# Cross-attention in fp32 on one core: the first batch loads half of x1 ahead of x2, projects queries ahead of keys, gives every strip of its first scores its own banks, and takes block 11 out of PSUM ahead of T4 and the reciprocal

## The chip, the cores and the metric

The kernel runs on one core of one Trainium2 chip. A core has five engines that run side by side and wait for one another by semaphores: TensorE (PE in the profile; its weight loads are PEld), VectorE (DVE), ScalarE (ACT), GpSimd (POOL) and SyncE (SP), which here only issues DMAs. The metric is the device time of one execution in microseconds (us). The kernel before takes 721.2 us, the median of three runs (721.2 to 721.28).

## What is computed

For each of 8 batches there are two inputs of 512 channels by 1024 positions, `x1` and `x2`. All numbers are fp32.

```python
q = einsum('bcn,dc->bnd', x1, Wq) + bq          # 64 features a position
k = einsum('bcn,dc->bdn', x2, Wk) + bk[:, None]
v = einsum('bcn,dc->bdn', x2, Wv) + bv[:, None]  # 512 channels
attn = softmax(einsum('bnd,bdm->bnm', q, k), axis=2)
return einsum('bcm,bnm->bcn', v, attn) + x1
```

## The kernel before

**The order of the sums.** Since each row of `attn` sums to one, the kernel multiplies `x2` by the unnormalised exponentials first (stage y), divides by the row sums, then multiplies by `Wv` (stage o), and adds `bv` and `x1` on the way out. Both products are cut into 2 by 2 blocks and made with seven block products in place of eight. That costs sums of blocks on DVE: `S1` to `S4` of the left factor (`left_sums`, L100) and `T1` to `T4` of the right factor (`right_sums`, L236). A product accumulates in two pairs of PSUM banks, `a0, a1` and `c0, c1` (table `MULT`, L259). Products 1, 6 and 5 leave their running sum in SBUF as well (tiles `u`, L289). A result block is taken out of PSUM by `evict_y` (L294): for block 11 DVE adds bank pair `c` and `u1` (L303), then multiplies by the reciprocal of the row sums (L306).

**PSUM.** There are eight banks of 128 partitions by 512 numbers: the two pairs `a` and `c`, and two tiles of two banks each in the pool `ps_s`, which serve the scores and the projections in turn.

**The scores.** For each half `h` of the 512-position halves of the queries, `scores` (L164) makes four strips `i` of keys; a strip is two matmuls into a `ps_s` tile or into a named pair of banks. ACT copies each strip to SBUF tile `e` (L187 for a named pair, two copies of 512; L189 for a `ps_s` tile, one copy of 1024). DVE folds the four strips into a running maximum (`fold`, L201), folds the two key halves (L205), and POOL reduces over the partitions (`highest`, L210). DVE then subtracts and ACT takes exponentials. The sums of the exponentials go the same way: folds on DVE, `total` on POOL (L215), the reciprocal on DVE (`shares`, L219).

**The first batch.** `head` (L345) does alone what later periods do for the next batch beside the products. It starts ten warming matmuls on zeros, then loads `wqk`, the four channel chunks of `x2` (L371), and `x1` in four pieces (`load_x1`, L357: two chunks of one position half each). Next come `keys` (bank `c0`), `head_queries` for half 0 (bank `c1`), the loads of `wvT` from ACT's queue (`load_values`, L89), the scores of half 0, the block sums S1 and S2, the queries and scores of half 1, and the exponentials of half 0. Strips 0, 1 and 3 of half 0 use `ps_s`, strip 2 uses pair `a`; DVE folds strips 1 and 3 straight from PSUM.

**The period of batch 0.** `period` (L428) runs product 1 (`first(1)`), finishes the scores of half 1, and then follows a written order: T1, T2, the row sums of half 0, T4, product 2, the reciprocal of half 0, the keys of batch 1, block 11 out of PSUM, and so on. Later, `scores_and(n, 0, "c", ...)` puts strip 2 of the next batch's scores into pair `c`, which block 11 must have left.

**What sets the order.** The kernel is under a manual schedule: each engine runs its instructions in the order in which the code writes them, and waits only for what an instruction reads or overwrites. SP and ACT each have a DMA queue of their own. A DMA also waits on its issuing engine where the semaphore it is given still serves an earlier transfer.

Of the kernel before, what the change touches and what calls it, by code (L numbers as in the profile page):

```python
# [15 lines left out]
def kernel(  # L16
# [69 lines left out]
    def load_values():  # L86
        for r in range(2):
            for k in range(2):
                nc.scalar.dma_start(w[f"{r + 1}{k + 1}"], wvT[r, k])  # L89

    def left_sums(a, *ks):

# [24 lines left out]
    def load_a(s, *ks):  # L117
        for k in ks:
            s.a[k] = sb.tile(
                [P, MH, C // 2], F32, tag=f"a{k}", name=f"a{k}_{s.b}", bufs=1 + (k[0] == "2")  # L120
            )
            nc.sync.dma_start(s.a[k], x2T[s.b, int(k[0]) - 1, int(k[1]) - 1])
# [35 lines left out]
    def keys(s, bank=None):  # L158

        ps = project(s, "k", wk_sb, bank)  # L160
        s.k = sb.tile([P, H], F32, tag="k", name=f"k_{s.b}", bufs=2)
        nc.scalar.activation(s.k, ps, AF.Identity, bias=bk_sb)
# [31 lines left out]
    def fold(s, h, i, kind, op, ps=None):  # L194

        e = s.e[h]
        if i == 1:
            s.mx[h] = sb.tile([P, 2, H], F32, tag="fold", name=f"{kind}_{s.b}_{h}", bufs=2)
        f = s.mx[h]
        new = e[:, :, i, :] if ps is None else ps  # L200
        nc.vector.tensor_tensor(f, e[:, :, 0, :] if i == 1 else f, new, op)  # L201
# [5 lines left out]
    def highest(s, h):  # L207
        fold_halves(s, h, ALU.max)
        s.top[h] = sb.tile([P, H], F32, tag="top", name=f"top_{s.b}_{h}", bufs=2)
        nc.gpsimd.partition_all_reduce(s.top[h], s.mx[h][:, 0, :], P, ReduceOp.max)  # L210
# [6 lines left out]
    def shares(s, h):  # L217
        s.rden[h] = s.den[h]
        nc.vector.reciprocal(s.rden[h], s.den[h])  # L219
# [25 lines left out]
    def sum_e(s, *ks):  # L245
        for i in (0, 2):
            part = {n: v[:, i : i + 2, :] for n, v in s.t.items()}
            for k in ks:
                right_sums(part, k)
# [41 lines left out]

    RESULT = {"11": ("c", 1), "22": ("c", 5), "12": ("a", None), "21": ("c", 6)}

    def evict_y(s, k):  # L294
        bank, add = RESULT[k]
        rden = s.rden[int(k[1]) - 1]
        y = s.y[k] = sb.tile([P, 2, H], F32, tag=f"y{k}", name=f"y{k}_{s.b}")
        for j in range(2):
            ps = s.bank[bank, j]
            if add is None:  # L300
                nc.vector.tensor_tensor(y[:, j, :], ps, rden, ALU.mult)
            else:
                nc.vector.tensor_tensor(y[:, j, :], ps, s.tmp[add, j], ALU.add)  # L303
        if add is not None:
            for j in range(2):
                nc.vector.tensor_tensor(y[:, j, :], y[:, j, :], rden, ALU.mult)  # L306

    def fetch_o(s, k):

# [25 lines left out]
    def head_queries(s, x_sb, h, bank):  # L335

        ps = ps_a.tile([P, H], F32, tag=bank, name=f"ps_q_{s.b}_{h}")
        for c in range(CT):
            for r in (lo, hi):
                nc.tensor.matmul(  # L340
                    ps[r, :], wq_sb[:, c, :], x_sb[:, c, ts(h, H)], start=(c == 0), stop=(c == CT - 1)
                )
        nc.scalar.activation(s.q[:, ts(h, H)], ps, AF.Identity, bias=bq_sb)  # L343

    def head(s):  # L345

        s.q = sb.tile([P, N], F32, tag="q", name=f"q_{s.b}", bufs=2)
        x1_sb = sb.tile([P, CT, N], F32, tag="x", name="x1_head")
        x2_sb = sb.tile([P, 2, MH, H], F32, tag="e1", name="x2_head")
        s.x = x2_sb.rearrange("p a (b t) n -> p (a b) (t n)", t=2)

        def load_x1(queue, c, h):
            queue.dma_start(  # L357
                x1_sb[:, c : c + 2, ts(h, H)],
                x1[s.b, c * P : (c + 2) * P, ts(h, H)].rearrange("(t p) n -> p t n", p=P),
            )  # L360

        nc.gpsimd.dma_start(bqk_sb, bqk)
        nc.gpsimd.dma_start(bv_sb, bv)
        nc.scalar.dma_start(wqk_sb, wqk)
        warm = const.tile([P, P], F32, name="warm")
        nc.vector.memset(warm, 0.0)
        ps = ps_a.tile([P, H], F32, tag="a0", name="ps_warm")
        for _ in range(WARM):
            nc.tensor.matmul(ps[:, 0:P], warm, warm, start=True, stop=True)
        for c, queue in ((0, nc.sync), (1, nc.sync), (2, nc.scalar), (3, nc.sync)):  # L370
            queue.dma_start(s.x[:, c, :], x2[s.b, ts(c, P), :])  # L371
        load_x1(nc.scalar, 0, 0)
        load_x1(nc.sync, 2, 0)
        nc.scalar.activation(warm[:, 0:1], warm[:, 0:1], AF.Exp)
        load_a(s, "11")
        load_x1(nc.sync, 0, 1)
        load_x1(nc.sync, 2, 1)
        load_a(s, "21", "22", "12")
        keys(s, "c0")
        head_queries(s, x1_sb, 0, "c1")  # L380
        load_values()
        copies = [scores(s, 0, i, "a" if i == 2 else None) for i in range(MH - 1)]
        for copy in copies:
            copy()
        fold(s, 0, 1, "max", ALU.max, copies[1].ps)
        copy = scores(s, 0, 3)
        fold(s, 0, 3, "max", ALU.max, copy.ps)
        copy()
        fold(s, 0, 2, "max", ALU.max)
        highest(s, 0)  # L390
        sum_a(s, "S1", "S2")
        head_queries(s, x1_sb, 1, "c0")
        load_x(states[1], x1)
        copies = [scores(s, 1, 0), scores(s, 1, 1), scores(s, 1, 2, "c")]
        for g in range(2):
            for i in range(MH):
                first_exponentials(s, g, i)
        for copy in copies:
            copy()
        fold(s, 0, 1, "sum", ALU.add)  # L400
        fold(s, 0, 2, "sum", ALU.add)
        fold(s, 1, 1, "max", ALU.max)
        fold(s, 0, 3, "sum", ALU.add)
# [24 lines left out]
    def period(s, n, nn, nnn):  # L428

        def first(i):
            multiply(s, "y", i, s.a, s.t, MH)

        def second(i):
            multiply(s, "o", i, w, s.y, 2)

        open_t(s)
        first(1)
        if s.b == 0:  # L440
            head_second(s, n)
        sum_e(s, "T1", "T2")
        if s.b == 0:
            total(s, 0)
        sum_e(s, "T4")
        if n:
            load_a(n, "11")
        first(2)
        shares(s, 0)
        if s.b == 0:  # L450
            keys(n)
            load_x(nn, x1)
        evict_y(s, "11")
        sums(s, 1)
        sum_e(s, "T3")
        shares(s, 1)
        if n:
            load_a(n, "12", "21", "22")
        first(6)

        def next_queries():
            queries(nn)
            load_x(nn, x2)

        def next_keys():
            keys(nn)
            if nnn:
                load_x(nnn, x1)

        if n:  # L470
            scores_and(n, 0, "c", next_queries if nn else nothing)
            for i in range(1, MH):
                fold(n, 0, i, "max", ALU.max)
            highest(n, 0)
            if s.b == 0:
                left_sums(w, "S1", "S2", "S3", "S4")
        first(5)
        fetch_o(s, "11")
        fetch_o(s, "22")
        if n:  # L480
            for i in range(MH):
                exponentials(n, 0, i)
            if s.b:
                sum_a(n, "S1", "S2", "S3")
        first(7)
        evict_y(s, "22")
        first(3)
        evict_y(s, "12")
        if n:
            scores_and(n, 1, "a", next_keys if nn else nothing)  # L490
            sums(n, 0)
        sum_y(s, "T1")
        sum_y(s, "T2")
        if n:
            sum_a(n, *(("S4",) if s.b else ("S1", "S2", "S3", "S4")))
            for i in range(1, MH):
                fold(n, 1, i, "max", ALU.max)
            highest(n, 1)
        first(4)
        evict_y(s, "21")  # L500
        second(1)
        sum_y(s, "T3")
        sum_y(s, "T4")
        second(6)
        fetch_o(s, "12")
        if n:
            exponentials(n, 1, 0)
            exponentials(n, 1, 1)
        second(2)
        evict_o(s, "11")  # L510
        fetch_o(s, "21")
        second(5)
        if n:
            exponentials(n, 1, 2)
            exponentials(n, 1, 3)
        second(7)
        evict_o(s, "22")
        if n:
            second(3)
            evict_o(s, "12")  # L520
            second(4)
            evict_o(s, "21")
        else:
            second(4)
            evict_o(s, "21")
            second(3)
            evict_o(s, "12")
# [37 lines left out]
```

## Time and profile before

| what | us |
|---|---|
| median of three runs | 721.2 |
| the profiled execution, its own time | 720.54 |
| its span, first to last instruction | 718.5 |
| PE busy, of the span | 706.5 |
| DVE busy, of the span | 591.7 |
| POOL busy, of the span | 98.4 |
| TensorE clock granted, mean | 0.999 of full |

The page was taken from one profiled execution. Its time is 2.04 us more than its span; this is what lies before the first and after the last instruction. A busy engine is not the bound by that alone: what counts is which stretch an engine stands idle in, and what ended the wait. In a timeline line, the first number is the start, the second the busy time of the merged instructions, and the bracket holds the idle time of the engine before them with the instruction or transfer that ended it. The DMA engines move 332 GB/s on average in the first 16 us, and the loads of the first batch keep them busy until about 22 us.

### The profile page before, as it was taken

The numbers are of one execution on the slowest core, as the hardware profiler recorded it, in microseconds if no ns is written. First come the engines' busy times: TensorE is split into PE (matmuls) and PEld (weight loads), VectorE is DVE, ScalarE is ACT, GpSimd is POOL, SyncE is SP. The second block draws the span as 40 slices with busy tenths as digits, with TensorE's granted clock in tenths as the row PEclk, the third lists the DMA queues.
The fourth block names the chain that finished last, engine by engine and source line by source line (L and its number), as shares of the span: only waits on it lengthen the run. The fifth ranks groups of instructions, "written<-read, shape, count | busy, mean of one in ns | idle before, by whom it ended". The sixth has DMA issues, their size and how long they took to land.

```text
span 718.5 us, 5410 instructions
## 1 busy us (share of the span) xinstructions
PE 706.5 (98%) x1892; PEld 299.3 (42%) x1892; DVE 591.7 (82%) x569; ACT 201.6 (28%) x270; POOL 98.4 (14%) x38
## 2 busy tenths in 40 slices
PE   7899999999999999999999999999999999999997
PEld 3333444434444444444344443443434444444443
DVE  0999999887969889798887988879887898989444
ACT  2644323033230432115221242312324033230010
POOL 0124120030300302002110202002020020301100
PEclk9999999999999999999999999999999999999999
DMA  9566332243433413435033351332601350042003
GB/s 340 201 194 236 126 146 103 92 149 111 146 118 136 144 56 146 147 117 190 12 136 145 118 191 69 116 136 90 219 0 59 117 176 0 0 157 78 0 1 146
DMA packets 34699, 87.39 MB, mean 122 GB/s; under 512 B 3953, under 2 KB 3953, under 8 KB 34673
## 3 DMA queue, kind: packets, MB, share of 16 engines
q1 hardware_dynamic: 32352, 82.85, 32.8%
q10 hardware_dynamic: 2256, 4.20, 1.7%
q8 instruction: 15, 0.25, 0.1%
q14 instruction: 12, 0.09, 0.1%
q0 software_dynamic: 64, 0.00, 0.0%
HBM read 68.42 MB, written 16.78 MB: 119 GB/s over the span
## 4 chain that ended last, share of the span: by engine, by line
PE 86%; DVE 8%; DMA 3%; issue 1%; ACT 1%; ACTq 0%; DVEq 0%
PE ps_ya L279 27%; PE ps_yc L279 20%; PE ps_oa L279 14%; PE ps_oc L279 12%; PE ps_s L180 5%; PE ps_q L138 3%; PE ps_k L138 2%; DVE max L201 2%; DMA x_head<-in_x_dram 1%; DVE e L230 1%; DVE eT L236 1%; DMA o<-in_x_dram 1%; DVE aS L100 1%; PE ps_sc L180 1%; PE ps_sa L180 1%
## 5 line engine op out<-in xcount | busy, mean ns | idle before, releaser
L215 POOL PARTITION_ALL_REDUCE den<-sum x16 | 66.2, 4136 | 431.7 <-DVE sum L205 431.7
L279 PE MATMUL ps_ya<-eT,aS 128*128 128x512 f32 x256 | 113.1, 595 | 0.0
L279 PE MATMUL ps_yc<-e,a 128*128 128x512 f32 x256 | 112.6, 592 | 0.0
L289 ACT COPY uy<-ps_ya 128x512 f32<-128x512 f32 x48 | 28.1, 588 | 231.2 <-PE ps_ya L279 231.2
L230 DVE TENSOR_TENSOR e<-e,top 128x1024 f32<-128x1024 f32 x60 | 69.9, 1216 | 11.9 <-POOL top L210 11.9
L279 PEld LDWEIGHTS ps_ya<-eT,aS 128*128 128x128 f32 x256 | 48.0, 190 | 63.8 <-issue 62.8
L279 PEld LDWEIGHTS ps_yc<-e,a 128*128 128x128 f32 x256 | 48.6, 190 | 61.6 <-issue 60.1
L320 DVE SCALAR_TENSOR_TENSOR o<-ps_oc,bv_sb,o 128x512 f32<-128x512 f32 x48 | 35.8, 749 | 42.2 <-PE ps_oc L279 42.0
L231 ACT ACTIVATE e<-e 128x1024 f32<-128x1024 f32 x60 | 62.3, 1056 | 25.3 <-DVE e L230 23.5
L189 ACT COPY e<-ps_s 128x1024 f32<-128x1024 f32 x48 | 47.5, 1025 | 63.4 <-PE ps_s L180 61.8
L289 ACT COPY uo<-ps_oa 128x512 f32<-128x512 f32 x48 | 28.1, 585 | 131.0 <-PE ps_oa L279 127.7
L279 PE MATMUL ps_oc<-y,w 128*128 128x512 f32 x128 | 57.6, 593 | 0.3 <-DVE y L306 0.3
L279 PE MATMUL ps_ya<-e,a 128*128 128x512 f32 x128 | 56.3, 593 | 1.3 <-ACT e L225 1.3
L279 PE MATMUL ps_oa<-yT,w_S 128*128 128x512 f32 x128 | 57.5, 592 | 0.0
L279 PE MATMUL ps_yc<-eT,a 128*128 128x512 f32 x128 | 57.0, 598 | 0.0
L279 PE MATMUL ps_ya<-e,aS 128*128 128x512 f32 x128 | 56.2, 592 | 0.0
L219 DVE RECIPROCAL den<-den 128x512 f32<-128x512 f32 x16 | 53.6, 3349 | 0.0
L180 PE MATMUL ps_s<-q,k 64*128 64x512 f32 x192 | 49.5, 607 | 1.6 <-ACT q L343 1.6
L210 POOL PARTITION_ALL_REDUCE top<-max x16 | 30.6, 1914 | 135.5 <-DVE max L205 135.5
L303 DVE TENSOR_TENSOR y<-ps_yc,uy 128x512 f32<-128x512 f32 x48 | 31.1, 674 | 15.9 <-PE ps_yc L279 15.9
L201 DVE TENSOR_TENSOR sum<-sum,e 128x1024 f32<-128x1024 f32 x32 | 39.2, 1225 | 2.1
L201 DVE TENSOR_TENSOR max<-max,e 128x1024 f32<-128x1024 f32 x31 | 38.0, 1225 | 3.1
(66 smaller groups left out, 758.5 us busy)
## 6 DMA issues: line engine op xcount, KB each, us to landing
x_in_x_dram<-in_x_dram SPq DMA_DIRECT2D x56, 512.0 KB, 5.6
a<-in_x2T_dram SPq DMA_DIRECT2D x32, 512.0 KB, 4.3
o<-in_x_dram SPq DMA_DIRECT2D x64, 256.0 KB, 6.5
out_dram<-o SPq DMA_DIRECT2D x64, 256.0 KB, 2.1
x_head<-in_x_dram SPq DMA_DIRECT2D x6, 512.0 KB, 8.8
q<-q ACTq DMA_DIRECT2D x14, 128.0 KB, 7.2
x_head<-in_x_dram ACTq DMA_DIRECT2D x2, 512.0 KB, 8.5
w<-in_wvT_dram ACTq DMA_DIRECT2D x4, 256.0 KB, 5.6
```

What stands on the lines that cost most here:

```text
L138: nc.tensor.matmul(ps[r, :], w_sb[:, c, :], s.x[:, c, ts(h, H)], start=(c == 0), stop=(c == CT - 1),)
L180: nc.tensor.matmul(ps[g], s.k[r, ts(i, P)], s.q[r, ts(h, H)], start=True, stop=True)
L189: nc.scalar.copy(e[:, :, i, :], whole)
L201: nc.vector.tensor_tensor(f, e[:, :, 0, :] if i == 1 else f, new, op)
L215: nc.gpsimd.partition_all_reduce(s.den[h], s.mx[h][:, 0, :], P, ReduceOp.add)
L219: nc.vector.reciprocal(s.rden[h], s.den[h])
L230: nc.vector.tensor_tensor(e, e, top, ALU.subtract)
L231: nc.scalar.activation(e, e, AF.Exp)
L279: nc.tensor.matmul(ps, left[ka][:, k, ts(j, P)], right[kb][:, k, :], start=opens and k == 0, stop=i in (2, 3, 4) and k == n_k - 1, skip_gr ...
L289: nc.scalar.copy(s.tmp[i, j], ps)
L303: nc.vector.tensor_tensor(y[:, j, :], ps, s.tmp[add, j], ALU.add)
L320: nc.vector.scalar_tensor_tensor(o, s.bank[bank, j], bv_sb[:, c : c + 1], o, ALU.add, ALU.add)
```

## The change

Four things are edited, all of them in the first batch.

- `load_values` issues the four `wvT` loads on SP instead of ACT, and is called ahead of the projections.
- `head` loads half 0 of `x1` ahead of `x2`, deals the chunks of `x2` out to SP and ACT in turn, and projects the queries of half 0 ahead of the keys.
- The strips of half 0 go to `ps_s`, `ps_s`, pair `a` and pair `c`. The copy of strip 1 on ACT moves behind those of strips 2 and 3; DVE folds strip 1 from PSUM after the first copy, then strips 2 and 3 from SBUF. The queries of half 1 go to bank `a0` instead of `c0`.
- In the period of batch 0, the keys of batch 1 and the next load of `x1` are written ahead of DVE's work; DVE takes block 11 out of PSUM (the sums with `u1`), then makes T4, then the reciprocal, and then multiplies block 11 by it. `evict_y` gets a list of steps for this. Other batches keep their order.

```diff
@@ load_values
-                nc.scalar.dma_start(w[f"{r + 1}{k + 1}"], wvT[r, k])
+                nc.sync.dma_start(w[f"{r + 1}{k + 1}"], wvT[r, k])
@@ evict_y
-    def evict_y(s, k):
+    def evict_y(s, k, steps=(1, 2)):
+
         bank, add = RESULT[k]
-        rden = s.rden[int(k[1]) - 1]
-        y = s.y[k] = sb.tile([P, 2, H], F32, tag=f"y{k}", name=f"y{k}_{s.b}")
-        for j in range(2):
-            ps = s.bank[bank, j]
-            if add is None:
-                nc.vector.tensor_tensor(y[:, j, :], ps, rden, ALU.mult)
-            else:
-                nc.vector.tensor_tensor(y[:, j, :], ps, s.tmp[add, j], ALU.add)
-        if add is not None:
+        rden = s.rden.get(int(k[1]) - 1)
+        if 1 in steps:
+            s.y[k] = sb.tile([P, 2, H], F32, tag=f"y{k}", name=f"y{k}_{s.b}")
+        y = s.y[k]
+        for step in steps:
             for j in range(2):
-                nc.vector.tensor_tensor(y[:, j, :], y[:, j, :], rden, ALU.mult)
+                ps = s.bank[bank, j]
+                if add is None:
+                    if step == 1:
+                        nc.vector.tensor_tensor(y[:, j, :], ps, rden, ALU.mult)
+                elif step == 1:
+                    nc.vector.tensor_tensor(y[:, j, :], ps, s.tmp[add, j], ALU.add)
+                else:
+                    nc.vector.tensor_tensor(y[:, j, :], y[:, j, :], rden, ALU.mult)
@@ head
-        for c, queue in ((0, nc.sync), (1, nc.sync), (2, nc.scalar), (3, nc.sync)):
-            queue.dma_start(s.x[:, c, :], x2[s.b, ts(c, P), :])
         load_x1(nc.scalar, 0, 0)
         load_x1(nc.sync, 2, 0)
+        for c, queue in ((0, nc.sync), (1, nc.scalar), (2, nc.sync), (3, nc.scalar)):
+            queue.dma_start(s.x[:, c, :], x2[s.b, ts(c, P), :])
...
         load_a(s, "21", "22", "12")
+        load_values()
+        head_queries(s, x1_sb, 0, "c1")
         keys(s, "c0")
-        head_queries(s, x1_sb, 0, "c1")
-        load_values()
-        copies = [scores(s, 0, i, "a" if i == 2 else None) for i in range(MH - 1)]
-        for copy in copies:
-            copy()
+        copies = [scores(s, 0, i, bank) for i, bank in enumerate((None, None, "a", "c"))]
+        copies[0]()
         fold(s, 0, 1, "max", ALU.max, copies[1].ps)
-        copy = scores(s, 0, 3)
-        fold(s, 0, 3, "max", ALU.max, copy.ps)
-        copy()
+        for i in (2, 3, 1):
+            copies[i]()
         fold(s, 0, 2, "max", ALU.max)
+        fold(s, 0, 3, "max", ALU.max)
         highest(s, 0)
         sum_a(s, "S1", "S2")
-        head_queries(s, x1_sb, 1, "c0")
+        head_queries(s, x1_sb, 1, "a0")
@@ period
         if s.b == 0:
             total(s, 0)
-        sum_e(s, "T4")
+        else:
+            sum_e(s, "T4")
         if n:
             load_a(n, "11")
         first(2)
-        shares(s, 0)
         if s.b == 0:
             keys(n)
             load_x(nn, x1)
-        evict_y(s, "11")
+            evict_y(s, "11", (1,))
+            sum_e(s, "T4")
+            shares(s, 0)
+            evict_y(s, "11", (2,))
+        else:
+            shares(s, 0)
+            evict_y(s, "11")
```

## The prediction

> **What bounds the kernel now.** I read the busy time by stages first, because the page's average (PE 98% busy) hides where PE stands idle. The columns are the stage, its length, and the busy time of PE, PEld, DVE, ACT and POOL.
>
> ```profile
> core 0: us, PE busy (x) PEld busy (x) DVE busy (x) ACT busy (x) POOL busy (x), PEclk, DMA share, GB/s
> 0.00:16.00 16.00, 11.79 (x53) 5.78 (x53) 0.17 (x1) 2.86 (x4) 1.60 (x6) 1.00 0.89 332
> 16.00:28.23 12.23, 10.13 (x44) 3.60 (x45) 8.81 (x9) 5.29 (x8) 2.68 (x1) 1.00 0.80 289
> 28.23:52.09 23.86, 23.67 (x71) 8.73 (x72) 23.50 (x24) 15.17 (x21) 2.69 (x1) 1.00 0.49 158
> 52.09:110.43 58.34, 56.97 (x159) 23.18 (x157) 57.40 (x52) 18.88 (x25) 16.16 (x5) 1.00 0.48 167
> 110.43:714.40 603.97, 603.96 (x1568) 258.06 (x1568) 501.07 (x486) 159.44 (x214) 75.28 (x26) 1.00 0.31 107
> 714.40:718.50 4.10, 0.00 (x0) 0.00 (x0) 0.75 (x1) 0.00 (x0) 0.00 (x0) 0.90 0.39 146
> ```
>
> From 110.43 to 714.40 PE has no idle time. All that can be won lies before 110.43: 16.00 − 11.79 = 4.21 us, then 2.10, 0.19 and 1.37. Next I read PE's timeline for what ended those waits.
>
> ```profile
> 1.05 4.04 PE L369 MATMUL ps_warm<-warm 128*128 128x128 f32 x20 [1.05 <-DVE warm L366]
> ...
> 11.56 3.65 PE L340 MATMUL ps_q<-x_head,wqk_sb 128*64 128x512 f32 x16 [0.61 <-DMA x_head<-in_x_dram]
> 16.00 1.99 PE L180 MATMUL ps_s<-q,k 64*128 64x512 f32 x8 [0.79 <-ACT q L343]
> ...
> 28.23 7.13 PE L279 MATMUL ps_ya<-e,a 128*128 128x512 f32 x16 [1.31 <-ACT e L225]
> ...
> 60.99 1.29 PE L180 MATMUL ps_sc<-q,k 64*128 64x512 f32 x3 [0.90 <-DVE y L303]
> ```
>
> Two more waits follow, 0.17 us at 90.03 and 0.31 us at 110.43, both for DVE (L301, L306). The chain of waits says why: from 17 to 110 us it runs mostly over DVE, and DVE is busy 57.40 of 58.34 us in the fourth stage. So **up to 16 us the loads bound the kernel, then DVE's backlog until 110.43, then PE.** A PE wait that goes before 110.43 is a gain only if DVE also gets through earlier; otherwise PE waits at 90.03 or 110.43 instead.
>
> **Part 1: loads and projections.** Before, the keys are done as chunks land, and the queries wait for `x1`: they start at 11.56, ACT starts on them at 15.26 for 0.69, and scores start at 16.00. Afterwards one piece of `x1` is first on SP, the other second on ACT behind `wqk`. By packets, the two queues share evenly: from 3 to 5 us q1 (SP) moved 154 packets and q10 (ACT) 132, but 0.57 MB against 0.24 MB, as SP's were 4 KB and ACT's 2 KB; from 9.5 to 10.5, both at 2 KB, it was 0.20 against 0.20 MB. The Trainium skill (DMA: Bandwidth & Descriptors, Queues, rings and completion order) has the engines alternate between queues by packet, which fits. It also says under "Issuing engines are not separate DMA queues" that issuing from several engines saves only issue time. By that rule dealing `x2` to both queues gains nothing; by the rows it decides who is first, since packet size weighs. I take the rows. Both queues have moved 0.13 and 0.01 MB by 3.0 us. At 0.20 MB/us SP has its 0.524 MB at 4.97. ACT then has 0.40 of the 0.786 MB it needs, and gets a third of 0.40 MB/us against SP's 4 KB packets: 0.386 / 0.133 = 2.9 us, so 7.87. A landing follows the last byte by 0.5 (before, ACT's first 0.786 MB were moved at 7.85 and landed at 8.34): 8.36. The queries start at 8.40, 3.16 us earlier.
>
> But the keys now stand behind them. Sixteen matmuls, from the row's starts (0.48 after the first, then 0.427) and 0.59 for the last, end 7.05 us later, and ACT starts 0.05 after: 15.50. Adding 0.69 and 0.05, **scores start at 16.24, 0.24 later than now.** The last chunk of `x2` comes at about 13.5 by the same shares, and is needed at 14.4, so it hides with 0.9 to spare. The bound of this step: 0.5 either way for the landing (16.24 ± 0.5).
>
> `load_values` takes 1.80 us of ACT's queue away (15.27 to 17.07). Nothing is gained: the first score copy starts at 17.18, when its matmuls end. On SP the four issues go ahead of the next batch's `x1`, which waits for the queries of half 1 (23.33) anyway. SP's issues can wait for semaphores of earlier transfers, but those land by about 20. The `w` tiles are read at 79.10, so the cover is wide; if SP were late, the next `x1` landed at 31.9 and is used at 36.35: 4 us of slack.
>
> **Part 2: the strips.** Let S be the start of the scores. Now ACT copies strips 0 and 1 (17.18, 1.93 us), and DVE's first fold starts at 19.13 = S + 3.13, since it waits for ACT to leave strip 1's banks. Afterwards it follows copy 0 alone: S + 1.18 + 0.97 = S + 2.17. Strip 2's two copies (0.55 each, the first when its matmul ends, S + 2.45) end at S + 3.58. Fold 2 is then at S + 3.60, fold 3 one pace of 1.33 later, the fold of halves another 1.26: S + 6.19, against 23.05 = S + 7.05. **Gain 0.86.** Strip 3's copies (to S + 4.7) and strip 1's (to S + 5.7) hide under the queries of half 1; bank `a0` is free at S + 3.0 and needed at S + 3.6. POOL's reduction, S1, S2 and the exponentials follow in unchanged order, so `first(1)` starts 0.86 − 0.24 = 0.62 earlier. PE is ready then: its scores end at 26.91 + 0.24 = 27.15, and 28.23 − 0.62 = 27.61. DVE's backlog moves by 0.62 with it.
>
> **Part 3: block 11.** No instruction is added or dropped; five groups change places on DVE.
>
> ```profile
> 52.69 4.40 DVE L236 TENSOR_TENSOR eT<-e,eT 128x1024 f32<-128x1024 f32 x2
> 52.86 4.14 POOL L215 PARTITION_ALL_REDUCE den<-sum  x1 [10.36 <-DVE sum L205]
> ...
> 57.03 3.35 DVE L219 RECIPROCAL den<-den 128x512 f32<-128x512 f32 x1
> 60.30 1.22 DVE L303 TENSOR_TENSOR y<-ps_yc,uy 128x512 f32<-128x512 f32 x2
> ```
>
> T4's two instructions take 4.40 us where two such take 2.44 elsewhere: single records show 1.22 and 3.26, so the second loses 2.04 us to POOL. At 108.50 the two additions of a PSUM bank take 1.28 while POOL's reduction (108.75, 1.78) runs, and that reduction is as long as with DVE idle. So the block's additions should pass beside POOL where T4 does not. Where a 1024-wide sum is in flight at POOL's start, POOL takes longer (2.68 against 1.78 for the maximum), as if each held the other out. From that: POOL holds DVE for 2.0 us, starting at 53.0 when nothing is in its way. Additions 52.69 to 53.97; T4's first waits to 55.0 and ends at 56.2, the second at 57.3; reciprocal to 60.6; products to 61.8. Now the next fold starts at 62.65, then at 61.73. **Gain 0.92 on DVE**; bounds 0.0 (additions slowed as T4 is) and 1.2 (T4 not held at all). I take 0.92, as the row at 108.50 is the nearest.
>
> PE no longer waits 0.90 at 60.99, arrives 0.90 earlier at 90.03 and 110.43, and finds DVE 0.92 earlier: the small waits stay as they are. So PE's and DVE's gains are the same time, not two. The keys of batch 1 and `load_x`, written earlier, pass only DVE instructions: PE's, ACT's and SP's own orders do not change (16 matmuls, one activation, four DMAs), and POOL's queue has nothing between.
>
> **The sum:** −0.62 − 0.92 = −1.5 us. Span 718.5 to 717.0, the execution's own 720.54 to 719.0; the median is 0.66 us above the profiled execution, and 721.2 becomes **719.7**.
>
> **A rule against it.** PE now idles from 5.09 to 8.40, 3.3 us, where the longest gap was 1.34. The row: after the last matmul (714.39) the granted clock falls to half at 717.69, 3.3 us later; it rose at 4.30, 3.25 us after the first. The Trainium skill (TensorE: Matmul & The Clock Gate, What's actually happening) has a free-running window of 3.4 us, and an idle one halves the clock. The full-clock stretch, 713.39 us, is 209 such windows, so edges lie at 4.30, 7.71 and 11.13; the window up to 7.71 has 0.79 us of warming in it. By the rule it isn't idle and the sum stands; by the bare 3.3 us of the row the clock falls, the queries run at half speed for one window, and 1.6 us go.
>
> **Rivals.**
> - *Clock down for one window:* −1.5 + 1.6, 721.3. For: the gap is as long as the one at the end. Against: the 0.79 us. 0.15.
> - *Clock down for two windows,* through queries and keys: 3.4 us lost, 723.1. This is the slower side; it decides once PE loses over 3 us before the scores, as would a landing of `x1` at its old 11.51. 0.13.
> - *Block 11 gains nothing,* POOL holding the additions as well: −0.6, 720.6. 0.10.
> - *`x1` lands at 7.5 and T4 is held less:* −2.6, 718.6. 0.12.
> - *As summed,* 719.7 ± 0.6: 0.50.
>
> 0.2% is 1.44 us, about what a measurement can tell: faster means below 719.76. The main case gives 0.27 faster and 0.23 same; with 0.12 from the early case, faster is 0.39. Same: 0.23 + 0.10 + 0.11 of the one-window case = 0.44. Slower: 0.13 + 0.04 = 0.17. The range, 718.9 to 721.6, leaves out the two-window case and the ends.
>
> **What would show it.** Queries at about 8.4 with matmuls 0.43 apart (0.85 if the clock fell) and scores at 16.2; the first fold 2.2 us after them, `first(1)` at 27.6; the additions of block 11 at 0.6 to 0.7 each under POOL's reduction, no PE wait for L303, and the small waits at L301 and L306 still there. A clock below full before 16 us, a late `x2` chunk, or additions of 2 us would prove the sum wrong.

## The result and the profile after

The changed kernel takes 724.14 us, the median of six runs (723.28 to 724.74), against 721.2 before (six runs, 720.78 to 721.59). The ratio is 1.004, with a 95% interval of 1.0027 to 1.0053: 0.4% slower, where 719.7 was forecast. The profiled execution took 724.10 us, its span is 722.1; before it was 720.54 and 718.5. Four of the six executions show a mean granted clock of 0.995 and took 724.1 to 724.7; the other two show 0.999 and took 723.3 and 723.4, still over 2 us more than before. The trace is of one of the four, so where the other two lose is not shown.

The first view is again the busy time by stages. The stages are cut at the same events as before: the start of the scores, of product 1, of DVE's fold of the row sums ahead of T4, and of the product that follows PE's last wait.

```profile
core 0: us, PE busy (x) PEld busy (x) DVE busy (x) ACT busy (x) POOL busy (x), PEclk, DMA share, GB/s
0.00:20.47 20.47, 14.32 (x52) 7.45 (x52) 0.17 (x1) 2.86 (x4) 1.59 (x6) 0.83 0.91 338
20.47:32.22 11.75, 10.13 (x44) 3.60 (x44) 8.82 (x9) 5.35 (x9) 2.68 (x1) 1.00 0.47 157
32.22:56.08 23.86, 23.79 (x71) 8.91 (x72) 23.51 (x23) 15.17 (x21) 2.69 (x1) 1.00 0.50 163
56.08:113.62 57.54, 55.95 (x159) 22.72 (x157) 56.57 (x52) 18.48 (x25) 15.26 (x5) 1.00 0.47 169
113.62:717.60 603.98, 603.95 (x1568) 258.06 (x1568) 501.10 (x486) 159.34 (x214) 75.24 (x26) 1.00 0.31 107
```

By length, the first stage grew from 16.00 to 20.47 us (+4.47), the second shrank from 12.23 to 11.75 (−0.48), the third did not move, and the fourth shrank from 58.34 to 57.54 (−0.80). The fifth is the same to 0.01 us; the tail grew by 0.4. So the two parts on DVE gained, and apart from the tail everything that was lost was lost before the scores. The clock column says where to look: 0.83 in the first stage.

PE's timeline of the changed kernel:

```profile
1.04 4.47 PE L373 MATMUL ps_warm<-warm 128*128 128x128 f32 x20 [1.04 <-DVE warm L370]
9.84 6.42 PE L344 MATMUL ps_q<-x_head,wqk_sb 128*64 128x512 f32 x16 [4.33 <-DMA x_head<-in_x_dram]
16.08 3.62 PE L138 MATMUL ps_k<-x_head,wqk_sb 128*64 128x512 f32 x16
20.47 1.99 PE L180 MATMUL ps_s<-q,k 64*128 64x512 f32 x8 [0.78 <-ACT k L162]
...
93.21 1.29 PE L180 MATMUL ps_sa<-q,k 64*128 64x512 f32 x3 [1.27 <-DVE y L306]
```

Two things are new. PE waits 4.33 us for `x1`, which lands at 9.71. And the same sixteen query records that took 3.65 us before take 6.42. In the keys after them the pace is normal again. The rows below show why. They are cut where the recorded clock changes, at 5.21, 8.62 and 15.45 us. The first two changes are 3.41 us apart and the last two twice that, so the cuts are made every 3.41 us; the stretches between them are called windows here.

```profile
1.79:5.20 3.41, 3.41 (x18) 3.41 (x17) 0.00 (x0) 1.28 (x1) 0.85 (x2) 1.00 0.84 231
5.21:8.61 3.40, 0.30 (x3) 0.11 (x1) 0.00 (x0) 0.20 (x1) 0.00 (x0) 1.00 1.02 393
8.63:12.03 3.40, 2.19 (x6) 0.86 (x8) 0.00 (x0) 0.00 (x0) 0.00 (x0) 0.50 1.03 417
12.04:15.43 3.39, 3.39 (x10) 1.06 (x8) 0.00 (x0) 0.00 (x0) 0.00 (x0) 0.50 1.03 391
15.45:18.86 3.41, 3.41 (x18) 1.25 (x16) 0.00 (x0) 0.69 (x1) 0.00 (x0) 1.00 1.03 408
```

After the length, the first number is PE's busy time, and the third from the end is the granted clock. In the second window PE worked 0.30 of 3.40 us, and the clock is at half for the two windows that follow. It returns after the window in which PE was busy throughout; the one before it, with 2.19 of 3.40 us, did not bring it back. The 1.00 of the first row is no measurement, since the clock has no record before 5.21 us: its 18 warming records are the pace of half speed. The run with 28 warming matmuls, e1_bridge, passes 16 in the window before its first record (1.22 to 4.61) and 32 in the one behind it (4.63 to 8.03). Half speed ahead of the first record is thus not counted in the mean clock. The two executions at 0.999 may be ones in which the clock first rose during the queries; this is not shown.

### The profile page after: what moved, and what is told of

The parts are those of the page before. It is cut to its first block, busy times and chain, and to the rows that moved or that the text cites. A ratio compares the mean times of both kernels' runs of the same rounds, so it can differ in the third digit from the quotient of the medians.

```text
span 722.1 us, 5409 instructions
## 1 busy us (share of the span) xinstructions
PE 708.1 (98%) x1892; PEld 300.7 (42%) x1892; DVE 590.9 (82%) x569; ACT 201.2 (28%) x271; POOL 97.5 (13%) x38
## 4 chain that ended last, share of the span: by engine, by line
PE 86%; DVE 10%; issue 1%; DMA 1%; ACT 1%; ACTq 0%; DVEq 0%
PE ps_ya L279 27%; PE ps_yc L279 20%; PE ps_oa L279 14%; PE ps_oc L279 11%; PE ps_s L180 5%; PE ps_k L138 3%; PE ps_q L138 2%; DVE max L201 2%; DVE e L230 1%; DMA x_head<-in_x_dram 1%; DVE eT L236 1%; DVE aS L100 1%; PE ps_sa L180 1%; DVE den L219 1%; PE ps_q L344 1%
## 5 line engine op out<-in xcount | busy, mean ns | idle before, releaser
L180 PE MATMUL ps_s<-q,k 64*128 64x512 f32 x188 | 47.9, 608 | 1.6 <-ACT q L347 0.8
L308 DVE TENSOR_TENSOR y<-ps_yc,uy 128x512 f32<-128x512 f32 x48 | 31.2, 675 | 15.9 <-PE ps_yc L279 15.9
```

Of the source, the lines that this page charges most:

```text
L180: nc.tensor.matmul(ps[g], s.k[r, ts(i, P)], s.q[r, ts(h, H)], start=True, stop=True)
```

## The experiments

All of them were timed against runs of the kernel before on the same chip, which had medians of 720.8 to 720.9. Differences below are taken to those, unless another kernel is named.

**Each part alone.** Part 3 (block 11) and part 2 (strips), each put into the kernel before, and both together. Their diffs are the parts of the change shown above; nothing else is edited.

> The kernel before with part 3 alone (keys of batch 1 written earlier; block 11 out of PSUM, T4, reciprocal, products). My theory: DVE's next fold 0.8 earlier, the PE wait of 0.90 for L303 gone, 720.4 (0.1% faster). Rival (PE and DVE only swap waits, 1.27 us appears at L306): no gain, 721.2.

> The kernel before with part 2 alone (four pairs of banks for the strips, first fold after the first copy, queries of half 1 in bank a0). My theory: scores at 16.0 as before, fold of halves at 22.6 and first(1) at 27.75, 0.48 earlier, 720.7. Rival (strip copies in two pieces and the queries' new bank cost what the earlier fold gains): first(1) at 28.2, 721.2.

> The kernel before with parts 2 and 3, loads and projections untouched. If the gains add (both move DVE's backlog, which is the bound until 110 us): 0.48 + 0.82 = 1.3, so 719.9 and 0.18% faster. If they are the same time twice: 720.4. If the changed kernel's loss lies in these parts: 722 or more.

| run | us | against before | ratio, 95% interval |
|---|---|---|---|
| block 11 alone | 720.03 | −0.87 | 0.9989 (0.9982 to 0.9995) |
| strips alone | 720.37 | −0.53 | 0.9993 (0.9985 to 1.0001) |
| both | 719.59 | −1.31 | 0.9983 (0.9976 to 0.9989) |

The gains add: 0.87 + 0.53 = 1.40, measured 1.31. (The interval of the strips alone touches 1; that part rests on the sum and on the traces.) So they are not the same time counted twice. What the changed kernel loses, it loses in the rest, part 1 and the `wvT` loads: 724.14 − 721.2 + 1.31 = 4.25 us. This is a subtraction; part 1 was not run alone.

**The clock.** The changed kernel with more warming matmuls, so that PE is busy while it waits for `x1`: 28 in e1_bridge, 18 in e6_warm18, 22 in e10_warm22.

```diff
-    WARM = 10
+    WARM = 28
```

> The changed kernel with 28 warming matmuls in place of 10, so that PE stays busy until x1 lands at about 9.7. Clock theory (the half-speed queries, 9.84 to 16.08 where 3.5 us are enough, cost 2.8 us): clock full from about 5 us on, queries in 3.5 to 3.7 us, scores at about 17.7, time 2.8 below the changed kernel, about 721.3, the same as before within 0.2%. Landing theory (the late x1 and the last chunk of x2 at 14.5 set the end, the clock is hidden): scores stay at 20 or later and the time stays at about 724.

> The changed kernel with 18 warming matmuls: they end at about 7.2, PE then idles 2.5 to 3.3 us. If the clock falls only after a window with next to no PE work, it stays full and the time is that of the bridged kernel, 721.8. If a window that is mostly idle is enough, the queries run at half speed in some executions and the median is 722.5 or more.

> The changed kernel with 22 warming matmuls alone: the partner of the run with one-chunk pieces. Two-chunk pieces on both queues: x1 at 9.7 to 10.6 as in the three profiles so far, queries 0.9 to 1.8 us later than with one-chunk pieces and the time as much longer: 721.0 to 722.0. If the late landing was chance, both runs have the same time.

With 28 the time is 721.79 us (ratio to before 1.001, 1.0002 to 1.0018), with 22 it is 721.39 (1.0009, 1.0001 to 1.0017): 2.4 to 2.8 us below the changed kernel's 724.14, or 2.1 to 2.4 when each is taken against its own runs of the kernel before. In the trace with 28, `x1` came even later:

```profile
1.05 8.21 PE L373 MATMUL ps_warm<-warm 128*128 128x128 f32 x56 [1.05 <-DVE warm L370]
10.69 3.65 PE L344 MATMUL ps_q<-x_head,wqk_sb 128*64 128x512 f32 x16 [1.43 <-DMA x_head<-in_x_dram]
14.14 3.63 PE L138 MATMUL ps_k<-x_head,wqk_sb 128*64 128x512 f32 x16
18.55 1.99 PE L180 MATMUL ps_s<-q,k 64*128 64x512 f32 x8 [0.78 <-ACT k L162]
```

The queries take 3.65 us again and the scores start 1.92 us earlier than in the changed kernel, although the queries began 0.85 later. The profiled execution is 1.91 us shorter too (722.19 against 724.10). So the clock theory holds, though the scores came at 18.55 and not at 17.7, as `x1` landed later still. The landing theory falls as the whole of the cause: PE's time through the queries is not hidden by the last chunk of `x2`.

With 18 matmuls the median is 722.05 us (1.002, 1.0013 to 1.0027), but the 17 executions lie in groups from 721.1 to 723.8. The profiled one, at 723.51, bounds the share of work that keeps the clock:

```profile
6.93:10.33 3.40, 1.19 (x11) 1.00 (x9) 0.00 (x0) 0.20 (x1) 0.00 (x0) 1.00 1.04 414
10.35:13.74 3.39, 3.37 (x8) 1.11 (x10) 0.00 (x0) 0.00 (x0) 0.00 (x0) 0.50 1.02 402
13.76:17.16 3.40, 3.40 (x18) 1.24 (x16) 0.00 (x0) 0.69 (x1) 0.00 (x0) 1.00 1.05 399
```

A window in which PE was busy 1.19 of 3.40 us, 35%, was followed by half speed, though PE's gap inside it was only 2.25 us. In the kernel with both DVE parts (e4_both) a window of 1.71 of 3.40 us, 50%, was followed by full speed:

```profile
4.44:7.84 3.40, 1.71 (x10) 0.71 (x9) 0.00 (x0) 0.20 (x1) 0.00 (x0) 1.00 0.84 292
7.86:11.25 3.39, 2.94 (x12) 0.66 (x12) 0.00 (x0) 0.00 (x0) 0.00 (x0) 1.00 1.03 404
```

**The landing.** With the clock full, the changed kernel is still 1.9 to 2.2 us behind the two DVE parts (0.55 to 0.89 above the kernel before, against 1.31 below it), and its `x1` lands at 9.71, 10.55, 10.24 and 10.06 us in the four traces with 10, 28, 18 and 22 warming matmuls, where 8.36 was forecast. Two theories were tested: the form of the transfer (two chunks in one, on both queues at once) and the length of its rows.

```diff
-        load_x1(nc.scalar, 0, 0)
-        load_x1(nc.sync, 2, 0)
+        for c, queue in ((0, nc.scalar), (2, nc.sync), (1, nc.scalar), (3, nc.sync)):
+            queue.dma_start(x1_sb[:, c, ts(0, H)], x1[s.b, ts(c, P), ts(0, H)])
```

This is e5_pieces, with 28 warming matmuls, and e9_pieces22, with 22.

> The changed kernel with 28 warming matmuls, and half 0 of x1 in four transfers of one chunk (256 KB, still rows of 2 KB) instead of two of two chunks, two on each queue. Form theory (a transfer of two chunks starts slowly): queries start at about 8.4, time 2 us below the bridged kernel, 719.7. Row theory (rows of 2 KB are delivered at a limited number a microsecond at the start, whatever the form): queries start at 9.7 to 10.7, 721.3 to 722.

> The changed kernel with half 0 of x1 in four transfers of one chunk, and 22 warming matmuls, which end before x1 is there (in e5 the 28 ended at 10.4 and held the queries, though x1 had landed at 8.8). Form theory: the last piece lands at 8.8, queries start at about 8.9, scores at 16.7, time 719.9 to 720.3. Row theory: the last piece lands at 9.7 or later again and the time is 721 or more.

In e5_pieces the last piece lands at 8.77, but the time is 721.34 (1.0006, 0.9998 to 1.0014): in the profiled execution the clock rose late, at 7.06, so the warming ran to 10.41 and held the queries. With 22 the last piece lands at 8.76 and the time is 719.67 (0.9985, 0.9978 to 0.9991), 1.72 us below its partner e10_warm22. Here are the two, first with one-chunk pieces, then with two-chunk pieces.

```profile
8.50 3.65 PE L344 MATMUL ps_q<-x_head,wqk_sb 128*64 128x512 f32 x16
11.98 3.60 PE L138 MATMUL ps_k<-x_head,wqk_sb 128*64 128x512 f32 x16
16.38 1.99 PE L180 MATMUL ps_s<-q,k 64*128 64x512 f32 x8 [0.79 <-ACT k L162]
```

```profile
10.20 3.65 PE L344 MATMUL ps_q<-x_head,wqk_sb 128*64 128x512 f32 x16 [1.92 <-DMA x_head<-in_x_dram]
13.65 3.63 PE L138 MATMUL ps_k<-x_head,wqk_sb 128*64 128x512 f32 x16
18.06 1.99 PE L180 MATMUL ps_s<-q,k 64*128 64x512 f32 x8 [0.78 <-ACT k L162]
```

The scores start 1.68 us earlier, which is the 1.72. Of the 1.70 us between the starts of the queries, 1.30 is the later landing (10.06 against 8.76); the rest is that with one-chunk pieces the first queries need not wait for the last piece. Same bytes, same rows, same queues: the form decides between these two. How it does so is not settled. What the traces show is a hole on ACT's queue behind `wqk`. These are the packets of the two queues (q1 is SP's, q10 ACT's; packets, MB, share of the DMA engines) from 4 to 5 us in the changed kernel:

```profile
q1 hardware_dynamic: 100, 0.20, 71.3%
q10 hardware_dynamic: 7, 0.01, 3.2%
```

Both pieces of `x1` had been issued by 1.65 us, yet ACT's queue moved 7 packets where SP's moved 100; the even share that the sum relied on had nothing to share. From 5 us on ACT's piece flowed. The other three traces of two-chunk pieces have the hole from 4.5 to 5.5 us, and the one-chunk traces do not have it. Here is that microsecond, first in e10_warm22 and then in e9_pieces22:

```profile
q1 hardware_dynamic: 141, 0.33, 88.0%
q10 hardware_dynamic: 37, 0.04, 13.2%
```

```profile
q10 hardware_dynamic: 117, 0.23, 58.1%
q1 hardware_dynamic: 89, 0.17, 48.0%
```

A two-chunk piece on ACT does not make the hole by itself. In e8_between, below, the same piece stands behind `wqk` on ACT, but SP's queue begins with whole rows of `x2`: in that microsecond ACT moved 49 packets against SP's 64, and the piece landed at 8.86.

The row theory was tried with whole rows of `x1`, with 28 warming matmuls. Two whole chunks are as many bytes as four half ones, so the queries of half 0 of batch 0 use chunks 0 and 1 twice and leave out chunks 2 and 3. This kernel does not compute the result, and serves for its time alone.

```diff
-                    ps[r, :], wq_sb[:, c, :], x_sb[:, c, ts(h, H)], start=(c == 0), stop=(c == CT - 1)
+                    ps[r, :], wq_sb[:, c, :], x_sb[:, c if h else c % 2, ts(h, H)], start=(c == 0), stop=(c == CT - 1)
...
-        load_x1(nc.scalar, 0, 0)
-        load_x1(nc.sync, 2, 0)
+        nc.scalar.dma_start(x1_sb[:, 0, :], x1[s.b, ts(0, P), :])
+        nc.sync.dma_start(x1_sb[:, 1, :], x1[s.b, ts(1, P), :])
...
-        load_x1(nc.sync, 0, 1)
+        load_x1(nc.sync, 2, 0)
```

> The changed kernel with 28 warming matmuls, and as many bytes of x1 ahead of x2, but as two chunks in whole rows of 4 KB instead of four chunks in half rows of 2 KB; batch 0's queries of half 0 use chunks 0 and 1 twice and leave out chunks 2 and 3. Row theory: x1 is there by 7.5 to 8.5, scores at 16.2 or PE-bound earlier, about 2 us below the bridged kernel. Queue theory (the piece behind wqk on ACT waits for the descriptors of SP's, whatever the rows): queries still start at 9.7 or later.

The time is 721.14 us (1.0005, 0.9997 to 1.0014) and the piece on ACT lands at 9.09, between what the two theories expected. The run is inconclusive on rows. With the same 28 warming matmuls, rows of 2 KB in one-chunk pieces landed earlier (8.77, e5_pieces) than rows of 4 KB, so long rows are not what an early landing needs.

**Another order.** Part 2 and part 3 kept, but `x1` between the chunks of `x2`, so that PE always has something to do. The edit is shown against the kernel before; the `wvT` loads stay on ACT.

```diff
-        for c, queue in ((0, nc.sync), (1, nc.sync), (2, nc.scalar), (3, nc.sync)):
-            queue.dma_start(s.x[:, c, :], x2[s.b, ts(c, P), :])
+        for c in (0, 1):
+            nc.sync.dma_start(s.x[:, c, :], x2[s.b, ts(c, P), :])
         load_x1(nc.scalar, 0, 0)
         load_x1(nc.sync, 2, 0)
+        for c, queue in ((2, nc.scalar), (3, nc.sync)):
+            queue.dma_start(s.x[:, c, :], x2[s.b, ts(c, P), :])
...
-        keys(s, "c0")
+        head_keys(0, 1)
         head_queries(s, x1_sb, 0, "c1")
+        head_keys(2, 3)
```

`head_keys` runs the matmuls of `keys` for the named chunks into bank `c0`; the activation follows the last. The second run has 14 warming matmuls in place of 10.

> Parts 2 and 3 with another order of loads and projections: x2 chunks 0 and 1, then half 0 of x1, then x2 chunks 2 and 3; keys of chunks 0 and 1, queries, keys of chunks 2 and 3. 4 KB rows are first and PE has work while x1 comes. My estimate from the queue shares: x1 at 8.8 and 9.9, queries 8.9 to 12.4, keys done at 14.1, scores at 14.9 to 15.7, so 0.5 to 1.3 us below parts 2 and 3 alone. Rival (ACT's queue again holds its x1 piece to 11 us): scores at 16.3 or later, no gain or a loss.

> The kernel of e8 with 14 warming matmuls in place of 10. In e8 two of eight executions took 719.8 at a mean clock of 0.997, as if the clock had fallen once. If a window less than half busy is the cause, four more warming matmuls (about 0.9 us) fill it: no such executions, median 718.7 to 718.9. If they delay the first keys, up to 0.5 us is lost.

The times are 718.82 us (0.9975, 0.9965 to 0.9985) and 718.28 (0.9967, 0.9954 to 0.9979): faster than both kernels. PE's timeline of the second:

```profile
6.72 1.94 PE L390 MATMUL ps_k_head<-x_head,wqk_sb 128*64 128x512 f32 x8
8.84 3.65 PE L344 MATMUL ps_q<-x_head,wqk_sb 128*64 128x512 f32 x16 [0.19 <-DMA x_head<-in_x_dram]
12.33 1.89 PE L390 MATMUL ps_k_head<-x_head,wqk_sb 128*64 128x512 f32 x8
15.00 1.99 PE L180 MATMUL ps_s<-q,k 64*128 64x512 f32 x8 [0.79 <-ACT k L399]
```

From 6.72 us PE stands idle only 0.19 us until the last key, and the scores start at 15.00, 1.0 us earlier than before and 1.4 earlier than in e4_both (16.36), which is the 1.31 us between them. The two executions of e8 at 719.8 and a clock of 0.997 have no counterpart in the five of e11. With so few executions, that the clock is their cause is not proven.

## Why the prediction was wrong

**What bounds the kernel** was read rightly: loads, then DVE's backlog, then PE. The PE-bound stage from 113.62 did not change.

**Part 1 failed, in two terms.** The forecast had queries at 8.40 and scores at 16.24; they came at 9.84 and 20.47.

The larger term is the clock, whose fall the sum put at nothing: 6.24 us from the first query to the first key, against 3.48 at full speed (8.50 to 11.98 in e9_pieces22), 2.76 us.

The landing term, "ACT then has 0.40 of the 0.786 MB it needs", was mis-sized by 1.44 us. ACT's queue did not get its even share at once, since its two-chunk piece stood still until 5 us: by then it had moved 0.27 MB. Counted over the whole queue, 0.786 MB were moved by about 8.6 us in place of 7.87, and the piece landed 1.1 us after that in place of 0.5. Why this lag grew is not shown.

1.44 + 2.76 = 4.20 of the 4.23 us by which the scores missed. The rest of the sum was sound: with pieces of one chunk and 22 warming matmuls the scores came at 16.38. That run, e9_pieces22, is 1.17 us below the kernel before (719.67 against 720.84), where 1.5 was forecast for the change, and no better than the two DVE parts alone (1.31 below). So queries ahead of keys, with the clock kept, gained nothing, as forecast.

**The rule against the change** was named and then set aside with the wrong reason: "the window up to 7.71 has 0.79 us of warming in it. By the rule it isn't idle and the sum stands". The prediction took a window with any work in it for one that keeps the clock. The window in question in the kernel before shows only that 55% is enough:

```profile
4.31:7.71 3.40, 1.85 (x11) 0.78 (x10) 0.00 (x0) 0.20 (x1) 0.00 (x0) 1.00 1.02 380
```

The runs show the rest: 35% is too little and 50% is enough. 0.79 us of a 3.41 us window is 23%, so by these shares the clock would have fallen at that window's end even with `x1` at 8.40. The rival "clock down for two windows" was the right one. It was priced at 3.4 us lost in queries and keys together. The clock took 2.76, in the queries alone, and the late landing came on top, so the time is 1.0 us above its 723.1. Its chance of 0.13 was too low.

**Part 2** was right in its mechanism and mis-sized: 0.86 forecast, 0.48 in the trace. The term was fold 2 at S + 3.60. It started at S + 3.98 (24.45 − 20.47), because ACT's first copy of strip 2 did not go when its own matmul ended but waited for the strip's second one (0.69 us of waiting for PE, until 23.35):

```profile
21.65 1.01 ACT L189 COPY e<-ps_s 128x1024 f32<-128x1024 f32 x1 [1.23 <-PE ps_s L180]
23.35 1.07 ACT L187 COPY e<-ps_sa 128x512 f32<-128x512 f32 x2 [0.69 <-PE ps_sa L180]
```

**Part 3** was right: 0.92 forecast, 0.80 in the trace, 0.87 measured alone. DVE and POOL of the changed kernel:

```profile
56.68 1.28 DVE L308 TENSOR_TENSOR y<-ps_yc,uy 128x512 f32<-128x512 f32 x2
56.86 3.24 POOL L215 PARTITION_ALL_REDUCE den<-sum  x1 [10.36 <-DVE sum L205]
57.88 3.43 DVE L236 TENSOR_TENSOR eT<-e,eT 128x1024 f32<-128x1024 f32 x2
61.24 3.34 DVE L219 RECIPROCAL den<-den 128x512 f32<-128x512 f32 x1
64.61 1.29 DVE L310 TENSOR_TENSOR y<-y,den 128x512 f32<-128x512 f32 x2
```

The additions pass beside POOL at full speed, POOL itself takes 3.24 us in place of 4.14, and T4 takes 3.43 in place of 4.40. The 2.0 us for which POOL was to hold DVE came out too. The first sum of T4 alone runs from 57.88 to 60.18, 1.08 us longer than the 1.22 of other such sums; so by estimate it got going at 58.96, 2.1 us after POOL's start. One step was wrong without cost: "the small waits stay as they are". The wait for the additions (L303 before) is gone, but the one for block 12's products (L301 before, L306 now) grew from 0.17 to 1.27. PE had gained 1.91 us, not 0.90: the projection behind these scores starts 33.35 us after product 1 (65.57 − 32.22) in place of 35.26 (63.49 − 28.23). As DVE sets the end of this stretch, only DVE's gain counted.

**The `wvT` loads** cost nothing that the trace shows: SP issued them from 12.64 to 15.95 us and nothing waited for them. They were not moved alone in any run.

## What to carry to other kernels

Before a reorder that lets PE wait for one early transfer, add up PE's work in each clock window across the gap, not the length of the gap. The edges of the windows move from one execution to the next, so take the window that holds the whole gap: 3.41 us less the gap is left of it. If that is less than half, which by estimate it is for gaps above 1.7 us, bridge the gap with warming matmuls or order the loads so that each landing gives PE something to do. With 22 warming matmuls the gap was 1.92 us, and one of 13 executions still took 723.5 at a clock of 0.997.

Price a transfer at the head of a queue from a transfer of the same form at the head of a queue, beside the same neighbour on the other queue, and not from its share in a full one. When DVE has a backlog, look for work that reads PSUM to put beside the start of a POOL reduction, in front of the sums that read SBUF twice.

## What the runs showed of the hardware

- **The clock follows the share of work in fixed windows.** Stretches at full clock are whole multiples of 3.413 us (one in the changed kernel before the fall, 209 in the kernel before, 713.39 us). A window with 9%, 35% or 37% of PE busy was followed by half speed (changed kernel, e6_warm18, the end of e8_between); one with 50% or 55% by full speed (e4_both, the kernel before). From half speed, windows with 64%, 72% and 76% did not bring it back (changed kernel, e6_warm18, e5_pieces; the last two stand before the first record, where half speed is read from the pace of the warming matmuls); those with 95% and more did. The edges lie elsewhere in each execution: the clock first rose between 4.28 and 7.06 us.
- **A reduction on POOL and a sum of two SBUF tiles on DVE hold each other out; additions from PSUM do not.** The reduction over the sums took 4.14 us behind a 1024-wide SBUF sum and 3.24 beside the additions. Width is not the reason: beside the shorter reduction over the maxima, a 512-wide SBUF sum took 1.41 us in place of 0.68 (L100 in the changed kernel, 0.46 us after POOL's start at 82.54), and a 512-wide addition from PSUM 0.68 (L308, 0.35 us after POOL's start at 111.93). The hold seems to last for the reduction's first part alone: products of two SBUF tiles at 112.88, 0.95 us after POOL's start, were not slowed (1.28 for two), and T4's first sum ended 0.09 us after the reduction, not a whole sum later.
- **Two transfers of two chunks, issued first on both queues,** left ACT's queue nearly still for about a microsecond; four of one chunk with the same bytes landed 1.3 us earlier (8.76 against 10.06). With whole rows of `x2` at the head of SP's queue, the same piece on ACT was not held (landed at 8.86 and 8.80 in e8_between and e11_between14). Why is open.
